# Attention with group norm on one core: every attention and q, k, v matmul in 64x64 quarters of the TensorE array

## The chip, the core and the metric

The kernel runs on one core of a Trainium2 chip. A core has TensorE (PE: matmuls, with weight loads on PEld), VectorE (DVE), ScalarE (ACT), GpSimd (POOL) and SyncE (SP, which issues most DMAs). They work side by side and wait for each other by semaphores. TensorE writes to PSUM[...]; the other data is in SBUF. The metric is the device time of the whole program in microseconds (us), lower is better; the result is the median of several runs.

## What is computed

The input x is 4 images of 512 channels and 48 x 48 = 2304 positions in float32. The reference, cut to its core:

```python
hn = _group_norm(x, gn_scale, gn_bias)            # 32 groups of 16 channels
qkv = jnp.einsum('oc,bchw->bohw', qkv_w, hn) + qkv_b[None, :, None, None]
qkv = qkv.reshape(b, 3, num_heads, d, t).astype(jnp.float16)
q, k, v = (qkv[:, 0], qkv[:, 1], qkv[:, 2])       # 8 heads, d = 64, t = 2304
scale = jnp.asarray(1.0 / math.sqrt(math.sqrt(d)), dtype=jnp.float16)
w = jnp.einsum('bhct,bhcs->bhts', q * scale, k * scale)
w = jax.nn.softmax(w, axis=-1)
a = jnp.einsum('bhts,bhcs->bhct', w, v).astype(jnp.float32)
out = jnp.einsum('oc,bchw->bohw', proj_w, a) + proj_b[None, :, None, None]
return x + out
```

## The kernel before

All of the timed work is in `fast_path`; `general_path` runs only where a flag says that a softmax sum left its safe range, and it doesn't run here. The order of the instructions is written out by hand: `tc.manual_schedule` keeps each engine's instructions in the order in which Python issues them, and pools of buffers add the waits.

**Units, blocks and pairs.** Heads go in pairs, 4 pairs for each of 4 images, so 16 pairs `g`. The queries of a pair are cut into blocks `j` of 512, 512, 512, 512 and 256 (`QBLOCKS`). A *unit* is one key tile of 128 keys for both heads against a block of 512 queries (for the block of 256, two key tiles). A unit has two parts: the scores with their exponential (`scores`, lines 920 to 940), and the product with v (`values`, 942 to 966).

- Scores (L932): the two heads lie in rows 0 to 63 and 64 to 127 of q and k, so each unit has two matmuls with 64 rows and 128 columns of the array, one for each head, into the two PSUM banks of a `ps` tile. ScalarE makes exp of the whole tile, 128 x 1024, into `p` (L939). There are three `ps` tiles (six banks).
- Product with v (L957): two matmuls with 128 rows and 64 columns, one for each head, which add up all keys of a block in one bank `av`. At the block's end DVE copies it to `avx` (L966).
- Sums of p: DVE adds the p tiles of a block (`add`, L986, L989), two matmuls with ones add the rows up (`add_up`, L1009, tile `sl`, in the bank of `av`), DVE copies it (L1025), and over DMAs, GpSimd and DVE (`check_sums`, `invert`, `spread`, `divide`) the block becomes `att`, some steps later.

**Steps.** The stream is cut into bursts of three units (`BURST`), 27 per pair, 432 in all. The main loop makes one step for each burst:

```python
scores(stream[n])
if n > 0:
    add(stream[n - 1])
if summed:
    fill(n)
if n >= BEHIND:
    values(stream[n - BEHIND])
```

So a step has three scores, then the product with v of the burst two steps back, and then (or, where a sum is due, in between) `fill(n)`, which issues work from the list `beside`: the projections of q, k and v of later pairs, the output projection of the image before, and, by `do_tasks`, statistics and normalization of the next image on DVE. `fill` spends a credit that grows with the work left over the steps left, so that each piece comes before the pair that needs it.

**Chains.** A projection is a chain of matmuls that add up the four chunks of 128 input channels in one bank, which is then evicted.

- `qk_steps` (L709): for q or k, 512 positions at a time, float32; two matmuls per chunk with 128 rows and 64 columns, into the two halves of the partitions. DVE evicts with bias and scale (L719).
- `v_chain` (L760): for v, 128 positions by 256 columns, float32, two of them to a bank; DVE adds the bias (L768).
- `proj_chain` (L837): the output projection in float32r, 128 rows and 128 columns, twice (weights split in a high and a low part); DVE adds bias and residual (L864). ScalarE casts `att` to float32r first (`att32`, L831).

In the loop these chains share one bank (`pw`), in the start they use `ps` tiles. A float32 matmul of the program is two records in the trace.

**Start and end.** The first 78 us load and normalize x of image 0 and make q, k of pair 0 and v of the first four heads, with no attention beside them. The next image's x goes into the place of the old one (`reload`), two of its blocks into spare buffers (`SPARE`). At the end the last blocks' output projections are left over.

## Time and profile before

| | |
|---|---|
| Time of the kernel, median of 3 runs | 1618.18 us (1617.79 to 1618.43) |
| The profiled execution's own time | 1618.91 us |
| Its span, first instruction to last | 1617.1 us |
| Busy PE / PEld | 1583.4 / 695.5 us |
| Busy DVE / ACT / POOL | 1136.2 / 1282.8 / 298.4 us |
| First matmul; first score | 12.8 us; 77.8 us |
| exp (L939) | 1296 times, 1231.9 us busy |
| Scores (L932) and product with v (L957) | 2880 matmuls each, 359.5 and 361.0 us busy |
| q, k (L709) and v (L760) | 2464 and 2304 records, 519.3 and 268.6 us busy |
| Output projection (L837) | 624 records in the loop, 236.6 us busy |
| DMA, mean over the span | 51 GB/s |

How to read a line of the profile: the line of the code, the engine, the operation, out<-in by the program's names, for a matmul the rows*columns of the array that it uses, the shape, and xN for N instructions. Lists of groups then give busy us and mean ns of one, and after a second bar the idle time of the engine just before them, with what ended it (<-). A timeline line begins with its start and its busy time. Matmuls are pipelined, and their ends in the trace are modelled, so that the times of neighbours overlap: the distance from one start to the next says what a matmul costs.

### The profile page before, as it was taken

How to read it: one execution, taken by the hardware profiler on the slowest of the kernel's cores; microseconds unless marked ns; L12 is line 12 of the kernel's file. 1: busy time of each engine (PE TensorE's matmuls, PEld its weight loads, DVE VectorE, ACT ScalarE, POOL GpSimd, SP SyncE). 2: the span in 40 equal slices, each digit the busy share in tenths (PEclk: the TensorE clock that was granted, in tenths of full speed). 3: DMA queues.
4: the chain of work that ended last, by engine and by line, in shares of the span. 5: the costliest groups of instructions: out<-in, count | busy, mean ns of one | idle time of the engine just before them, and what ended most of it. 6: DMA issues, size and time to landing. Idle time of an engine off the chain costs nothing.

```text
span 1617.1 us, 28315 instructions
## 1 busy us (share of the span) xinstructions
PE 1583.4 (98%) x11500; PEld 695.5 (43%) x11500; DVE 1136.2 (70%) x1302; ACT 1282.8 (79%) x1398; POOL 298.4 (18%) x419
## 2 busy tenths in 40 slices
PE   6999999999999999999999999999999999999996
PEld 2533434443333534555333353455533334434544
DVE  6267668866666678986666666898666666767775
ACT  3077777888888888888887887887888888888894
POOL 1001102211121222212111121111211131111211
PEclk9999999999999999999999999999999999999999
DMA  7002020000000023511000002352100000016424
GB/s 221 1 14 66 11 64 24 18 14 11 14 18 14 12 65 118 154 54 28 14 11 18 14 12 61 100 158 73 31 14 12 14 18 15 15 24 191 121 62 132
DMA packets 94898, 82.11 MB, mean 51 GB/s; under 512 B 50852, under 2 KB 60964, under 8 KB 94756
## 3 DMA queue, kind: packets, MB, share of 16 engines
q1 hardware_dynamic: 92724, 78.35, 17.3%
q8 instruction: 92, 1.51, 0.4%
q10 hardware_dynamic: 1904, 1.84, 0.4%
q14 instruction: 50, 0.41, 0.1%
q0 software_dynamic: 128, 0.01, 0.0%
HBM read 60.70 MB, written 19.17 MB: 49 GB/s over the span
## 4 chain that ended last, share of the span: by engine, by line
PE 91%; ACT 4%; issue 2%; DVE 1%; DMA 1%; POOL 0%; SPq 0%; ACTq 0%; DVEq 0%; POOLq 0%
PE pqk L709 29%; PE ps L932 19%; PE av L957 19%; PE pv L760 16%; PE pr L837 7%; ACT p L939 3%; PE ps L709 1%; PE sl L1009 1%; ACT a L831 1%; DMA x<-x_dram 1%; DVE acc L986 0%; DMA sums<-slx 0%; DVE r L860 0%; DMA row<-inv 0%; DMA ib<-row 0%
## 5 line engine op out<-in xcount | busy, mean ns | idle before, releaser
L939 ACT ACTIVATE p<-ps 128x1024 f16<-128x1024 f32 x1296 | 1231.9, 1027 | 299.9 <-PE ps L932 299.3
L986 DVE TENSOR_TENSOR acc<-acc,p 128x3072 f16<-128x3072 f16 x270 | 485.3, 1798 | 75.5 <-ACT p L939 74.7
L709 PE MATMUL pqk<-x,wqkv 128*64 128x512 f32 (+1 forms) x2464 | 519.3, 551 | 0.0
L932 PE MATMUL ps<-q,k 64*128 64x512 f16 (+1 forms) x2880 | 359.5, 358 | 6.2 <-ACT p L939 5.3
L957 PE MATMUL av<-p,v 128*64 128x512 f16 (+1 forms) x2880 | 361.0, 364 | 0.4 <-DVE slx L1025 0.3
L760 PE MATMUL pv<-wqkv,x 128*64 128x256 f32 x2304 | 268.6, 380 | 0.0
L709 PEld LDWEIGHTS pqk<-x,wqkv 128*64 128x64 f32 x2464 | 168.9, 137 | 224.2 <-issue 166.8
L1047 POOL TENSOR_SCALAR in<-sums 128x8 f32<-128x8 f32 (+1 forms) x158 | 116.6, 738 | 795.0 <-DMA sums<-slx 788.7
L932 PEld LDWEIGHTS <-k 64*128 64x128 f16 x2880 | 107.3, 94 | 286.1 <-issue 238.1
L957 PEld LDWEIGHTS <-v 128*64 128x64 f16 x2880 | 131.9, 109 | 210.8 <-issue 166.6
L1073 POOL TENSOR_TENSOR att<-avx,ib 128x512 f16<-128x512 f32 (+1 forms) x78 | 120.0, 1539 | 450.4 <-DMA ib<-row 406.3
L760 PEld LDWEIGHTS pv<-wqkv,x 128*64 128x64 f32 x2304 | 160.1, 137 | 92.8 <-issue 4.5
L986 DVE TENSOR_TENSOR acc<-p,p 128x3072 f16<-128x3072 f16 x79 | 138.2, 1749 | 0.0
L837 PE MATMUL pr<-a,whi 128*128 128x512 f32 (+1 forms) x312 | 122.2, 399 | 4.6 <-DVE r L860 3.2
L837 PE MATMUL pr<-a,wlo 128*128 128x512 f32 (+1 forms) x312 | 114.4, 373 | 0.0
L989 DVE TENSOR_TENSOR acc<-acc 128x1024 f16<-128x1024 f16 x156 | 108.4, 695 | 5.4
L719 DVE TENSOR_SCALAR q<-pqk,bqkv 128x512 f16<-128x512 f32 (+1 forms) x79 | 55.0, 696 | 80.4 <-PE pqk L709 79.8
L719 DVE TENSOR_SCALAR k<-pqk,bqkv 128x512 f16<-128x512 f32 (+1 forms) x75 | 52.2, 696 | 78.1 <-PE pqk L709 78.0
L768 DVE TENSOR_TENSOR v<-pv,bv 128x512 f16<-128x512 f32 x72 | 49.7, 691 | 81.1 <-PE pv L760 80.9
L966 DVE COPY avx<-av 128x512 f32<-128x512 f32 (+1 forms) x79 | 50.6, 641 | 66.4 <-PE av L957 66.4
L864 DVE SCALAR_TENSOR_TENSOR r<-pr,bproj,r 128x512 f32<-128x512 f32 (+1 forms) x80 | 54.9, 694 | 43.6 <-PE pr L837 43.0
L837 PEld LDWEIGHTS pr<-a,whi 128*128 128x128 f32 x312 | 58.5, 187 | 41.9 <-issue 18.7
(62 smaller groups left out, 448.8 us busy)
## 6 DMA issues: line engine op xcount, KB each, us to landing
r<-x_dram SPq DMA_DIRECT2D x72, 256.0 KB, 3.0
out_dram<-r SPq DMA_DIRECT2D x69, 256.0 KB, 2.1
ib<-row SPq DMA_DIRECT2D x126, 128.0 KB, 3.0
x<-x_dram SPq DMA_DIRECT2D x62, 256.0 KB, 4.3
x<-x_dram SPq DMA_DIRECT2D x16, 128.0 KB, 4.8
sums<-slx SPq DMA_DIRECT2D x128, 2.0 KB, 2.1
ib<-row SPq DMA_DIRECT2D x30, 64.0 KB, 3.0
wqkv<-qkv_wT_dram SPq DMA_DIRECT2D x2, 768.0 KB, 6.9
```

Source lines behind the costliest of these rows:

```text
L709: nc.tensor.matmul(pw[0][lo : lo + D, :n], wqkv[:, c, w0 + lo : w0 + lo + D], hn[b, c, j], start=(c == 0), stop=(c == NC - 1),)
L719: nc.vector.tensor_scalar(qk[g][part][:, o : o + n], pw[0][:, :n], bqkv[:, col : col + 1], SCALE, ALU.add, ALU.mult,)
L760: nc.tensor.matmul(pw[0][lo : lo + D, a, :], hn[b, c, i * P // QB][:, at + lo : at + lo + D], wqkv[:, c, 2 * C + half * C // 2 :][:, : C / ...
L837: nc.tensor.matmul(ps[:, :n], w[:, c, bass.ts(m, P)], at32[b, j, c], start=(i == 0), stop=(i == len(steps) - 1),)
L864: nc.vector.scalar_tensor_tensor(xt[:, i], places[i], bias, xt[:, i], ALU.add, ALU.add)
L932: nc.tensor.matmul(ps[:, h, a * n : (a + 1) * n], kt[rows, bass.ts(i, P)], qt[rows, o : o + n], start=True, stop=True,)
L939: nc.scalar.activation(pt[:, r], ps, AF.Exp)
L957: nc.tensor.matmul(av[0][lo : lo + D, :n], vv[b, pr // 2][:, i, pr % 2 * P + lo : pr % 2 * P + lo + D], pt[:, r, h, a * n : (a + 1) * n], ...
L986: nc.vector.tensor_tensor(t, before, pt, ALU.add)
L989: nc.vector.tensor_tensor(t[:, 0], t[:, 0], t[:, r], ALU.add)
L1047: nc.gpsimd.tensor_scalar(t, sm, limit, None, op)
L1073: nc.gpsimd.tensor_tensor(atts[g][:, o : o + n], avx.pop((g, j))[:, :n], ibs.pop((g, j))[:, :n], ALU.mult,)
```

## The change

The scores, the product with v and the projections of q, k and v all use the array in quarters of 64 rows and 64 columns. Of the two uses with more rows, the sums (`add_up`, 128 rows, 64 columns) and the output projection (128 x 128) stay as they were.

- **Scores**: four matmuls for a unit, each head's 128 keys in two halves of 64 (`score`). The `ps` tiles go from three to two.
- **Product with v**: four matmuls for a unit; the keys of a tile are cut into two halves, and each half of the rows adds up in its own bank, so `av` takes two banks. At the end of a block `join` copies one bank to `avx` on ScalarE and adds the other on DVE.
- **Chains of q, k and v** are 256 columns wide (`CW`), and each is cut in two by rows: in one *slot* it is run with rows 0 to 63 for all four chunks, in the next slot with rows 64 to 127, beside the first half of the next chain (`merged`, `slot`). Two banks, `pw0` and `pw1`, take turns. A chain without a partner is run alone; `settle` puts a small matmul and a DVE copy ahead of that.
- **Steps**: a step has at most one slot, cut in halves, and scores and products alternate unit by unit: score, product, score, product, half of the slot, score, product, rest of the slot. Where a sum is due it comes first, then two scores, half of the slot, the products. A burst has two or three units (`BURSTS`): 3, 3, 2, 3, 2, 3, 2 for a block of 512 queries, 2, 2, 2, 3 for one of 256; 511 steps in all. A whole output chain may take a slot.
- **Around it**: the sum, check, spread and divide of a block are due 3, 5, 7 and 9 steps after its last burst (`lag`). The next image's statistics are made from temporary loads (`stats_ahead`, in the buffers of `att32`), so its x is loaded twice and no spare buffers are needed. Casts are queued one by one (`do_cast`).

The diff, cut to what the text speaks of:

```diff
+BURSTS = {QB: (3, 3, 2, 3, 2, 3, 2), T % QB: (2, 2, 2, 3)}
+LAST_BURSTS = (3, 3, 3)
+CW = QB // 2
...
-    ps_s = ctx.enter_context(tc.tile_pool(name="ps_s", bufs=3, space=PSUM))
+    ps_s = ctx.enter_context(tc.tile_pool(name="ps_s", bufs=2, space=PSUM))
...
+    def chain_bank(name):
+        at = 1 - (last_bank[0] if held[0] is None else held[0])
+        last_bank[0] = at
+        return ps_w.tile([P, QB], F32, tag=f"pw{at}", name=name)
...
+        def step(c, row):
+            rows = rows_of_array(row)
             for lo in (0, D):
                 nc.tensor.matmul(
                     pw[0][lo : lo + D, :n],
-                    wqkv[:, c, w0 + lo : w0 + lo + D],
-                    hn[b, c, j],
-                    start=(c == 0),
-                    stop=(c == NC - 1),
+                    wqkv[rows, c, w0 + lo : w0 + lo + D],
+                    hn[b, c, j][rows, off : off + n],
+                    start=(c == 0 and not row),
+                    stop=(c == NC - 1 and row != 0),
                 )
...
+        ps = ps_s.tile([P, 2, QB], F32, tag="ps", name=f"ps_{g}_{j}_{k}_{r}")
+        for a in range(per):
+            i = (at + r) * per + a
+            for lo in (0, D):
+                for h in range(2):
+                    rows = slice(h * D, (h + 1) * D)
+                    nc.tensor.matmul(
+                        ps[lo : lo + D, h, a * n : (a + 1) * n],
+                        kt[rows, i * P + lo : i * P + lo + D],
+                        qt[rows, o : o + n],
...
+            for half in range(2):
+                keys = slice(half * D, (half + 1) * D)
+                for h in range(2):
+                    lo = h * D
+                    at_v = pr % 2 * P + lo
+                    nc.tensor.matmul(
+                        av[0][lo : lo + D, half, :n],
+                        vv[b, pr // 2][keys, i, at_v : at_v + D],
+                        pt[keys, r, h, a * n : (a + 1) * n],
...
+    def join(to, banks, n):
+        nc.scalar.copy(to, banks[:, 0, :n])
+        nc.vector.tensor_tensor(to, banks[:, 1, :n], to, ALU.add)
...
+        if before and not (chain and before.followed):
+            settle()
+            if not chain:
+                settle()
+        if chain:
+            chain.open()
...
+        steps = merged(chain, before)
+        yield from in_halves(steps, max(at + us for at, _, us, _ in steps) / 2)
+        pending[0] = chain
+        if before:
+            closed(before)
...
+        return ((3, 5, 7, 9) if stream[n][0] < NG - 2 else (3, 4, 5, 6))[step]
...
+        summed = list(blocks(n, 0))
+        for found in summed:
+            rows(*found, add_up(*found))
...
+        part = begin_slot(n)
         if summed:
-            rows(*summed, add_up(*summed))
...
+            issue([ss], 2)
+            if n > 0:
+                add(stream[n - 1])
+            if part:
+                next(part)
+            issue([vs], 2)
+            issue([ss, vs], 1)
+        else:
+            issue([ss, vs], 2)
+            if n > 0:
+                add(stream[n - 1])
+            if part:
+                next(part)
+            issue([ss, vs], 1)
+        in_order()
...
+        finish(part)
```

## The prediction

> **What bounds the kernel now.** I read the page first: the busy times, then the chain that ended last.

> ```profile
> PE 1583.4 (98%) x11500; PEld 695.5 (43%) x11500; DVE 1136.2 (70%) x1302; ACT 1282.8 (79%) x1398; POOL 298.4 (18%) x419
> ...
> PE 91%; ACT 4%; issue 2%; DVE 1%; DMA 1%; POOL 0%; SPq 0%; ACTq 0%; DVEq 0%; POOLq 0%
> ```

> TensorE is on 91% of the chain, so only its time counts: what its matmuls take and what lies between them. The timeline of PE over one step, with a block's sum (sl) in it, shows both (start, busy us):

> ```profile
> 601.74 0.82 PE L932 MATMUL ps<-q,k 64*128 64x512 f16 x6
> 602.49 0.84 PE L957 MATMUL av<-p,v 128*64 128x512 f16 x6
> 603.16 1.88 PE L709 MATMUL pqk<-x,wqkv 128*64 128x512 f32 x8
> 604.88 0.38 PE L1009 MATMUL sl<-acc,ones 128*64 128x512 f16 x2
> 605.20 0.82 PE L932 MATMUL ps<-q,k 64*128 64x512 f16 x6
> ```

> Busy times overlap, so I take differences of starts. At 2.4 columns per ns six score matmuls, two side by side, need 3 x 0.213 = 0.64 us, but the next run starts 0.75 later: 0.11 over. av to pqk: 0.67, 0.03 over. pqk (2 x 0.853 = 1.71) to sl: 1.72, nothing over. sl (0.21) to ps: 0.32, 0.11 over. So the array runs at full rate except where the number of rows changes, between 64*128 and 128*64; there it loses 0.11 us. f16 to f32 in one shape is nearly free. Such a pair of matmuls starts every 0.216 us.

> ScalarE over the same time, then PE and ScalarE where a step had no projection in it:

> ```profile
> 602.17 2.86 ACT L939 ACTIVATE p<-ps 128x1024 f16<-128x1024 f32 x3 [0.38 <-PE ps L932]
> ...
> 629.12 0.82 PE L957 MATMUL av<-p,v 128*64 128x512 f16 x6
> 629.87 0.89 PE L932 MATMUL ps<-q,k 64*128 64x512 f16 x4
> 631.28 0.39 PE L932 MATMUL ps<-q,k 64*128 64x512 f16 x2 [0.52 <-ACT p L939]
> 631.61 0.84 PE L957 MATMUL av<-p,v 128*64 128x512 f16 x6
> ```

> The first exp starts 0.43 after its score (602.17 - 601.74). Three take 2.86, the last alone 1.03, so one follows another by 0.915. A step of three without a projection is 1.3 us of PE against 2.75 of exps: PE waits for ScalarE (the 0.52), today seldom (12 waits, 5.3 us). Normally the projection's 1.7 us cover the exps, and three score buffers let PE run ahead.

> For the prices, DVE at a block's end and three rows of the groups by shape:

> ```profile
> 603.44 0.69 DVE L966 COPY avx<-av 128x512 f32<-128x512 f32 x1 [0.78 <-PE av L957]
> ...
> 605.30 0.69 DVE L1025 COPY slx<-sl 128x512 f32<-128x512 f32 x1
> ...
> L719 DVE TENSOR_SCALAR q<-pqk,bqkv 128x512 f16<-128x512 f32 x63 | 47.3, 750 | 71.6 <-PE pqk L709 71.1
> ...
> L831 ACT CAST a<-att 128x512 fp32r<-128x512 f16 x64 | 35.2, 639 | 2.7 <-POOL att L1036 2.3 <-PE pr L837 0.5
> ...
> L719 DVE TENSOR_SCALAR q<-pqk,bqkv 128x256 f16<-128x256 f32 x16 | 7.7, 480 | 8.8 <-PE pqk L709 8.7
> ```

> av is copied out by DVE alone, right after its last matmul and beside the next projection; the sum comes 1.4 us later and finds the bank free.

> [...]

> **Part by part.** The sum is made against the profiled run's 1618.9 us (span 1617.1, 1.8 around it), 0.7 above the median of 1618.2. Counts of the changed kernel come from the order in which it issues.

> 1. Shape changes of the array: 955 before, 400 after (what stays: whole projections of the output in 128*128, and the sums in 128*64). 555 x 0.115 = **-64**.

> 2. Matmul work. Scores and av become 11,520 quarter matmuls, four per unit instead of two per unit; 12,672 f32 records of 64x256, eight per chunk of two chains. If four quarters run at once, a score or av unit is 0.216 and a chain's slot 8 x 0.216 = 1.73, the same array time as now. Bounds: 0 if they overlap; 396 slots x 1.73 = +683 if the f32 row halves don't. I take 0: two tiles overlap fully now, in rows (ps) and in columns (av). Blocks of 256 queries have loads twice as dense as any seen: 0 to +61 (2304 x 0.107 / 4); I take 0. 128 of the f32 records run with the other half empty (a chain that has no partner): 128 x 0.213 / 4 = **+7**.

> 3. The end of a block. The step in which av's last matmul falls is now: score, av, score, av, half slot, score, half slot: 5 x 0.216 + 1.73 = 2.80 us. ScalarE has in its queue exp, exp, then the copy, then the third exp. Exp 1 starts at 0.43, exp 2 at 1.35, ending at 2.37; the copy (0.6, by the 0.639 of the cast) ends at 2.9, the DVE add (0.69) at 3.6 with handoffs. PE's next instruction is the sum, which takes av's banks, and nothing passes it: all later scores wait. It comes at 2.80 and waits 0.85. Before or after the short block (step of 2.59, or the copy behind three exps) it is 1.1: mean 0.95. It hits 79 blocks. Nine of these steps have no slot to cover any of it, 1.7 more each: 79 x 0.95 - 5 (slots of the output projection, longer) + 9 x 1.2 (a part is in point 4's kind of wait) = **+81**. Bounds: 0, if the copy gets ahead of exp 2, to +110.

> 4. Steps without a slot. 511 steps (17 of three units and 15 of two per head pair) hold about 396 slots of q, k, v and 71 steps with an output projection; 49 are empty, nine counted above. Score buffers fall from three to two. An empty step of three: 2.75 + 0.15 handoffs - 1.29 = 1.6; of two: 1.83 + 0.1 - 0.86 = 1.1. 28 x 1.6 + 12 x 1.1 = **+58**. The step before cannot lend time, as two buffers let ScalarE be at most two exps behind.

> 5. Banks of the chains. Two banks alternate; a chain's eviction (0.48 for 256 columns) must end before the slot after the next opens, 0.86 us into a step. On DVE it stands behind an add of up to 1.75 us, started only when the last exp of the step before is done, and a 0.63 task. 3.0 us of step usually hold 0.4 + 1.75 + 0.48, not with two tasks. Bounds 0 to +70 (0.7 in 100 steps); I take **+30**.

> 6. Engines that stay off the path: ScalarE +79 x 0.6 = +47 (1283 to 1330); DVE +56 (twice as many evictions at 0.48 instead of 0.75: 22 for q and k, 15 for v; 79 more adds: 19), to about 1190; 60 more loads of x on SP, hidden, since DMA is 17% busy. Waits of PE for exps that the kernel before has go: **-5**.

> Sum: 1618.9 - 64 + 7 + 81 + 58 + 30 - 5 = 1726; less 0.7, **1725**.

> **Rivals.**
> A, the forecast: PE saves 64 on shape changes and gives over twice that back in new waits; about 1725, by the bounds of 3 and 5 from 1650 to 1800.
> B, faster: the join and the exps don't hold PE. If the copy were done by 2.2 us into the step, point 3 is gone; if steps without a slot fall where ScalarE is idle anyway, most of 4. Then 1618.9 - 64 + 7 + 20 = 1582. The page speaks for it in that ScalarE is idle 299.9 us before exps today; against it, this idle time lies at the start of each step and the copy stands behind exps of the same step. It decides from waits below 57 us in all; I count 169.
> C: the f32 row halves run one after the other: 1725 + 683, less some 90 of waits that the longer slots cover: about 2320. For it: no trace shows four quarters. Against: both kinds of two-way tiling are at full rate.
> D: the quarters overlap but 256-column blocks are limited by loads, or halves start skewed: 1725 + 61 = 1786.
> E: gains and waits cancel, 1615 to 1621.

> **Numbers.** A 0.67, B 0.17, C 0.08, D 0.05, E 0.03. Faster by over 0.2% (what a measurement can tell here) 0.17, within 0.03, slower 0.80. A alone: 1650 to 1800. To leave out no more than 2 in 10, C and most of B, the range goes from 1600 to 1810.

> **What would show it.** In the changed trace: ps to av without the 0.11 (right for 1); a chain's slot of 1.73 in two halves of 0.86 (wrong at 3.4: C); PE idle before sl of 0.7 to 1.1, put down to DVE avx, some 75 us in all (3); PE idle before ps put down to ACT, 60 to 80 us (4); PE idle before pqk and pv put down to DVE (5). PE's share of the chain falls below 90%, and ACT and DVE rise. If sl starts within 0.2 us of the step's last matmul, point 3 is wrong, and the kernel is faster if 4 shrinks too.

## The result and the profile after

The changed kernel takes 1738.86 us (median of 4 runs, 1738.57 to 1743.03) against 1618.15 us, a ratio of 1.0752 with a 95% interval of 1.0733 to 1.0771: slower by 121 us. The profiled execution is the slowest of the four, 1743.03 us with a span of 1741.3.

The page of the changed kernel, busy times and the chain that ended last:

```profile
PE 1591.8 (91%) x25526; PEld 964.4 (55%) x25526; DVE 1185.0 (68%) x1586; ACT 1329.2 (76%) x1478; POOL 244.6 (14%) x419
...
PE 66%; DVE 13%; ACT 12%; issue 5%; DMA 2%; POOL 1%; SPq 0%; ACTq 0%; DVEq 0%; POOLq 0%
```

PE is busy for almost the same time as before (1583.4), but holds only two thirds of the chain; DVE and ACT have come onto it with 25%. So PE's work hasn't grown, it is waited for. Its timeline, from one full step to the next (start, busy us):

```profile
700.87 0.39 PE L943 MATMUL ps<-q,k 64*64 64x512 f16 x4
701.08 0.39 PE L970 MATMUL av<-p,v 64*64 64x512 f16 x4
...
701.51 0.39 PE L970 MATMUL av<-p,v 64*64 64x512 f16 x4
701.73 1.90 PE L710 MATMUL pqk<-x,wqkv 64*64 64x256 f32 x32
703.46 0.39 PE L943 MATMUL ps<-q,k 64*64 64x512 f16 x4
```

Four quarters run at full rate: a score and a product each take 0.21 from start to start, 32 float32 records 1.73. Nothing is lost between ps, av and pqk. What is lost stands in the list of PE's waits (us, times, longest):

```profile
PE ps L943 <- ACT p L950: 49.8, 111, 5.4
PE sl L1033 <- DVE avx L985: 41.3, 52, 2.6
...
PE pqk L710 <- DVE q L720: 8.4, 12, 2.4
PE pv L754 <- DVE v L763: 7.0, 14, 0.8
PE pr L852 <- DVE r L868: 5.4, 8, 1.3
```

These leave out part of each wait, since the ends of matmuls are modelled. I therefore measure *in starts*: the distance from one start to the next, less what the matmuls need at the rate of the traces (512 columns in 0.216 us, 2.4 per ns) and the 0.11 that a change of shape took in the trace before; what is over 0.2 us counts as a wait of the later matmul. "Chains" are pqk, pv, pr and settle together.

| waits of PE after 78 us, in starts | for exps (ps) | sl | chains | time, us |
|---|---|---|---|---|
| before | 8 | 0 | 6 | 1618 |
| changed | 80 | 47 | 51 | 1739 |
| 1 join on DVE | 79 | 14 | 48 | 1704 |
| 2 464 steps | 22 | 65 | 65 | 1717 |
| 3 add last | 228 | 92 | 32 | 1923 |
| 4 the three together | 162 | 150 | 40 | 1930 |
| 5 add last, some | 85 | 93 | 32 | 1765 |
| 6 products first | 89 | 8 | 50 | 1706 |
| 7 products first, 464 steps, add last | 24 | 100 | 31 | 1720 |
| 8 before with two score buffers | 473 | 0 | 3 | 2081 |
| 9 as 6, short adds last | 93 | 14 | 28 | 1692 |
| 10 as 9, 464 steps | 34 | 6 | 34 | 1634 |
| 11 as 10, projections later | 30 | 6 | 29 | 1626 |
| 12 as 11, last two pairs | 25 | 7 | 30 | 1624 |

A step without a slot, then a block's end, on PE, ScalarE and DVE of the changed kernel:

```profile
710.58 0.41 PE L943 MATMUL ps<-q,k 64*64 64x512 f16 x4 [0.48 <-ACT p L950]
...
715.45 0.41 PE L1033 MATMUL sl<-acc,ones 128*64 128x512 f16 x2 [0.47 <-DVE avx L985]
```

```profile
709.50 4.69 ACT L950 ACTIVATE p<-ps 128x1024 f16<-128x1024 f32 x5 [0.65 <-PE ps L943]
714.04 0.63 ACT L984 COPY avx<-av 128x512 f32<-128x512 f32 x1
```

```profile
714.70 0.69 DVE L985 TENSOR_TENSOR avx<-av,avx 128x512 f32<-128x512 f32 x1 [2.32 <-ACT avx L984]
```

ScalarE makes five exps without a pause while PE waits for buffers, and only then the copy; DVE has been idle for 2.32 us, adds for 0.69, and the sum starts. Through the whole run DVE waits 158.5 us in that place (79 times): nobody works there while the copy stands in ScalarE's queue.

### The profile page after: what moved, and what is told of

Its sections match the earlier page's. It is cut to its first block, busy times and chain, and to the rows that moved or that the text cites. A ratio compares the mean times of both kernels' runs of the same rounds, so it can differ in the third digit from the quotient of the medians.

```text
span 1741.3 us, 57021 instructions
## 1 busy us (share of the span) xinstructions
PE 1591.8 (91%) x25526; PEld 964.4 (55%) x25526; DVE 1185.0 (68%) x1586; ACT 1329.2 (76%) x1478; POOL 244.6 (14%) x419
## 4 chain that ended last, share of the span: by engine, by line
PE 66%; DVE 13%; ACT 12%; issue 5%; DMA 2%; POOL 1%; SPq 0%; ACTq 0%; DVEq 0%; POOLq 0%
PE pqk L710 22%; PE ps L943 12%; PE pv L754 12%; PE av L970 10%; ACT p L950 10%; PE pr L852 7%; DVE acc L1006 5%; DVE acc L1013 3%; DVE avx L985 2%; PE sl L1033 2%; ACT avx L984 1%; PE ps L710 1%; DMA ib<-row 1%; DMA r<-x_dram 1%; DVE r L868 1%
## 5 line engine op out<-in xcount | busy, mean ns | idle before, releaser
L710 PE MATMUL pqk<-x,wqkv 64*64 64x256 f32 (+1 forms) x8704 | 584.6, 381 | 14.5 <-DVE q L720 8.4
L943 PE MATMUL ps<-q,k 64*64 64x512 f16 (+1 forms) x5760 | 509.3, 362 | 50.4 <-ACT p L950 49.8
L1006 DVE TENSOR_TENSOR acc<-acc,p 128x2048 f16<-128x2048 f16 (+1 forms) x349 | 504.4, 1445 | 27.1 <-ACT p L950 26.8
L970 PE MATMUL av<-p,v 64*64 64x512 f16 (+1 forms) x5760 | 495.0, 359 | 1.2 <-DVE slx L1046 1.2
L710 PEld LDWEIGHTS pqk<-x,wqkv 64*64 64x64 f32 (+1 forms) x8704 | 325.1, 134 | 188.8 <-DVE q L720 33.1
L943 PEld LDWEIGHTS <-k 64*64 64x64 f16 x5760 | 193.5, 106 | 219.3 <-issue 136.3
L754 PE MATMUL pv<-wqkv,x 64*64 64x256 f32 (+1 forms) x4320 | 302.0, 379 | 10.7 <-DVE v L763 7.0
L754 PEld LDWEIGHTS pv<-wqkv,x 64*64 64x64 f32 (+1 forms) x4320 | 174.6, 133 | 101.4 <-DVE v L763 25.5
L970 PEld LDWEIGHTS <-v 64*64 64x64 f16 x5760 | 179.1, 108 | 92.6 <-issue 11.0
L985 DVE TENSOR_TENSOR avx<-av,avx 128x512 f32<-128x512 f32 (+1 forms) x80 | 51.1, 638 | 158.6 <-ACT avx L984 158.5
L1006 DVE TENSOR_TENSOR acc<-p,p 128x3072 f16<-128x3072 f16 (+1 forms) x79 | 130.1, 1647 | 0.0
```

Of the source, the lines that this page charges most:

```text
L710: nc.tensor.matmul(pw[0][lo : lo + D, :n], wqkv[rows, c, w0 + lo : w0 + lo + D], hn[b, c, j][rows, off : off + n], start=(c == 0 and not row),
L754: nc.tensor.matmul(pw[0][lo : lo + D, : C // 2], hn[b, c, j][rows, at + lo : at + lo + D], wqkv[rows, c, 2 * C + half * C // 2 :][:, : C / ...
L943: nc.tensor.matmul(ps[lo : lo + D, h, a * n : (a + 1) * n], kt[rows, i * P + lo : i * P + lo + D], qt[rows, o : o + n], start=True, stop=True,
L970: nc.tensor.matmul(av[0][lo : lo + D, half, :n], vv[b, pr // 2][keys, i, at_v : at_v + D], pt[keys, r, h, a * n : (a + 1) * n], start=(i = ...
L985: nc.vector.tensor_tensor(to, banks[:, 1, :n], to, ALU.add)
L1006: nc.vector.tensor_tensor(t[:, :m], before[:, :m], pt[:, :m], ALU.add)
```

## The experiments

My theory: three new waits, of the sum, of the score buffers and of the chains' banks, eat what the shape changes save. Rivals: DVE's or ScalarE's load; quarters that are slow in themselves; waits that only change places.

**1. The join's copy on DVE.**

```diff
-        nc.scalar.copy(to, banks[:, 0, :n])
+        nc.vector.tensor_copy(to, banks[:, 0, :n])
```

> The changed kernel with one word altered: the first half of join is copied on DVE instead of ScalarE, so that it doesn't stand behind an exp. Against the changed kernel's 1739 us. Theory (new waits at the block's end): PE's waits ahead of sl for DVE avx, about 47 us in starts over the block ends, go to under 10; DVE's 80 copies of 0.69 fall into its own idle time of 2 us there, so 1690 to 1705. Rival 1 (DVE is the engine that holds the kernel back): 55 us more on DVE, so 1745 or more. Rival 2 (waits only move: the exps of the same step are late instead): the waits for exps grow by what the sums lose, 1730 to 1740.

1704.21 us, ratio to the kernel before 1.0534 (1.0517 to 1.0552). sl's waits fall from 47 to 14, a little less than expected, and the others stay. With 47 us more on DVE (1185.0 to 1232.1) the kernel is 35 us faster, so rival 1 falls, and rival 2 for this wait.

**2. Fewer steps.**

```diff
-BURSTS = {QB: (3, 3, 2, 3, 2, 3, 2), T % QB: (2, 2, 2, 3)}
+SEVEN = (3, 3, 2, 3, 2, 3, 2)
+BURSTS = {j: SEVEN if j in (1, 3) else (3,) * 6 for j in range(4)}
+BURSTS[4] = (3, 3, 3)
```

> The changed kernel cut into 464 steps instead of 511: blocks 0, 2 and 4 of a pair in bursts of three units only. Steps without a slot of a chain fall from 49 to 13 (12 of three units), all in the last two pairs. Theory (a step without a slot leaves ScalarE behind, and two score buffers let PE get only two exps ahead): PE's waits for exps fall from 80 us in starts to some 25 to 35; 1739 - 50 = about 1690. A rival: the waits come from the two score buffers in every step, with or without a slot; then they stay at 80 or grow, since more of the steps have three units, 1735 to 1760. If the time is lost because the quarters themselves are slow, nothing changes either.

1716.60 us, 1.0609 (1.0591 to 1.0627). The waits for exps fall from 80 to 22 as expected, so they do come from steps without a slot. But 32 of the 58 us come back, in sl and in the chains:

```profile
PE sl L1035 <- DVE avx L987: 59.6, 56, 2.5
...
PE ps L945 <- ACT p L952: 12.0, 27, 1.3
```

A block that ends in a burst of three has its last product one half slot later in the step, and the copy behind it. The trace shows it by blocks: the sums of blocks 0 and 2, which now end so, wait 1.32 and 1.37 on average instead of 0.57 and 0.34, those of blocks 1 and 3, left as they were, 0.24 and 0.15 instead of 0.25 and 0.71. The rival is wrong, but what neither side expected is seen: a wait that goes uncovers another.

**3. The add behind the eviction.**

```diff
-            if n > 0:
+            if n > 0 and ended(n - BEHIND):
                 add(stream[n - 1])
...
         finish(part)
+        if n > 0 and not ended(n - BEHIND):
+            add(stream[n - 1])
```

> The changed kernel with DVE's add of the p tiles issued at the end of the step, behind the eviction of the chain that ends there, and not before it (in the step of a block's last product the order stays). Theory (chain banks wait for evictions that stand behind an add): PE's waits ahead of pqk, pv and pr, about 50 us in starts, fall to under 20; 1739 - 35 = about 1704. Rival: the evictions are late because DVE has too much to do or because the bank turns round too fast by itself; then 1735 to 1745, and the waits are still put down to q, k and v on DVE.

1922.95 us, 1.1886 (1.1867 to 1.1906): a miss of 220 us. The chains' waits fall from 51 to 32, but ScalarE has a wait that it didn't have (its list of waits):

```profile
ACT p L950 <- DVE acc L1006: 229.3, 79, 5.7
```

The first add of a block reads the p tiles of its first two bursts. Moved to the end of its step, it holds the first one so long that the fourth burst, which needs this buffer (there are three), waits 2.9 us, once in each block. My edit, not the theory, was at fault; I hadn't counted what the add frees.

**4. The three edits together.**

> All three edits in one kernel: join on DVE, 464 steps, add behind the eviction. Theory (three separate waits that add up): 1739 - 40 - 50 - 35 = about 1615, at or a little below the kernel before; a bit less if, as before, an overlap of the waits makes the sum smaller: 1600 to 1640. Rival (quarters are slower in themselves, or the waits feed on each other): above 1680.

1929.52 us, 1.1931 (1.1886 to 1.1977). It contains the edit of experiment 3 and shows no more than that; inconclusive on the sum of the three.

**5. The same, without the add that holds p.**

```diff
+    def soon_read(n):
+        return ended(n - BEHIND) or stream[n - 1][2] == 1
...
-            if n > 0:
+            if n > 0 and soon_read(n):
                 add(stream[n - 1])
...
         finish(part)
+        if n > 0 and not soon_read(n):
+            add(stream[n - 1])
```

> As the third experiment (DVE's add behind the eviction), but the add that reads the first two p tiles of a block stays where it was, as does the one in the step of a block's last product. In the third experiment ScalarE waited 229 us for DVE acc at 79 places, once for each block, because that add holds the first p tile and there are three. Theory: with that gone, what is left is the effect that was sought; PE's waits ahead of pqk and pv fall from 38 us in starts to 15, in 5 of 7 steps; 1739 - 20 = about 1719. Rival (p buffers are short also behind the other adds): ScalarE's waits for DVE acc stay above 30 us, 1740 to 1780.

1765.13 us, 1.0905 (1.0887 to 1.0923): again slower than the changed kernel, though ScalarE's wait for DVE is gone and the chains' waits are at 32. Now sl waits 93, at 78 of 79 places. Experiment 7 has the same edit and shows the cause best.

**6. The products first.** The copy stays on ScalarE, one place further ahead.

```diff
-            issue([ss, vs], 2)
+            if v and v[3]:
+                issue([ss], 1)
+                issue([vs], v[5])
+                issue([ss], 1)
+            else:
+                issue([ss, vs], 2)
```

> The changed kernel with one order altered: in the step of a block's last product, all products are issued after the first score, so that ScalarE has the copy of join behind one exp and not behind two. No work is added or moved to another engine. Theory (the copy's place in ScalarE's queue is what sl waits for): sl's waits, 47 us in starts, go to under 10, as with the copy on DVE; 1739 - 40 = about 1700. Rival (it is ScalarE's load: its exps are late in these steps, so the copy is late anywhere, or the exps behind it become late by 0.6 us): 1725 to 1740, with the waits for exps up by 20 to 40 us.

1706.21 us, 1.0542 (1.0524 to 1.0559), sl's waits at 8, exps' at 89. No work was taken from ScalarE, so it was the place in its queue; the rival's extra wait for exps is 9 us, not 20 to 40.

**7. Products first, 464 steps and the edit of 5.**

> The changed kernel with 464 steps, the products first in a block's last step, and the add behind the eviction where it holds no p tile. Theory: the three waits are separate once the join no longer depends on the burst's length; PE's waits for exps 22 us as in the second experiment, ahead of sl under 10, of the chains about 30: 1739 - 58 - 37 - 16 = about 1628, range 1605 to 1650; at or a little above the kernel before. Rival (each wait that goes lets another take its place): 1670 or more.

1720.50 us, 1.0634 (1.0616 to 1.0652), a miss. Waits for exps and chains came as expected (24 and 31), sl's are 100. DVE at the end of a block:

```profile
714.71 0.48 DVE L722 TENSOR_SCALAR q<-pqk,bqkv 128x256 f16<-128x256 f32 x1 [0.87 <-PE pqk L712]
715.11 1.98 DVE L1008 TENSOR_TENSOR acc<-acc,p 128x2048 f16<-128x2048 f16 x1
717.12 1.42 DVE L1015 TENSOR_TENSOR acc<-acc 128x1024 f16<-128x1024 f16 x2
718.46 0.68 DVE L987 TENSOR_TENSOR avx<-av,avx 128x512 f32<-128x512 f32 x1
```

Behind the eviction (714.71) now come 3.4 us of adds, and right after them, without a gap, the join's add. Moved out of the evictions' way, the adds stand in the join's way: in 74 of 76 waits of sl, such an L1015 stands directly ahead of the join. In the sixth kernel, where the adds stand in the old place, 33 waits of chains (21 us) have the same two short adds directly ahead of the eviction.

**8. The kernel before with two score buffers.**

```diff
-    ps_s = ctx.enter_context(tc.tile_pool(name="ps_s", bufs=3, space=PSUM))
+    ps_s = ctx.enter_context(tc.tile_pool(name="ps_s", bufs=1, space=PSUM))
...
-            ps = ps_s.tile([P, 2, QB], F32, tag="ps", name=f"ps_{g}_{j}_{k}_{r}")
+            ps = ps_s.tile([P, 2, QB], F32, tag=f"ps{turn()}", name=f"ps_{g}_{j}_{k}_{r}")
```

> The kernel before, whole, with scores in two ps tiles instead of three (the third tile is used at the start and the end alone). No quarters, no join, no new chains: the price of the third score buffer alone, in the order of three scores, then three products. The third score of a step then waits until the first exp of the step is done, about 0.43 + 1.03 us into it, 1.0 us later than before: with 432 steps up to 430 us, less where the exps of the step before ran late anyway. Theory (the number of score buffers sets how far PE may go ahead, and the changed kernel's alternation of score and product is what keeps its loss at 80): 1850 to 2050. Rival (two buffers are enough and the changed kernel's waits for exps come from its steps alone): below 1660.

2080.62 us, 1.2855 (1.283 to 1.2881), 30 us beyond the range. PE in one step:

```profile
802.49 0.61 PE L936 MATMUL ps<-q,k 64*128 64x512 f16 x4
804.05 0.39 PE L936 MATMUL ps<-q,k 64*128 64x512 f16 x2 [0.96 <-ACT p L943]
```

The third score starts 1.56 us after the first instead of 0.43: 1.1 us in each of 432 steps, 473 in all. The third buffer is worth 462 us in the old order. The changed kernel, whose second av bank and second chain bank take its place in PSUM, waits only 72 us more for exps than the kernel before. That this is because it alternates score, product and half slots fits these numbers, but no run changes the alternation alone.

**9. Only the short adds behind the eviction**, with the products first.

```diff
+            tails.append((t, parts))
+            acc[g, j] = [t[:, :1]]
...
+    def add_tails():
+        while tails:
+            t, parts = tails.pop()
             for part in parts:
                 nc.vector.tensor_tensor(t[:, 0], t[:, 0], part, ALU.add)
-            acc[g, j] = [t[:, :1]]
...
         finish(part)
+        add_tails()
```

> The sixth experiment (products first in a block's last step, copy on ScalarE) and one more order: the two or three short adds at the end of a block (128x1024, 0.71 us each) are issued at the end of their step, behind the eviction of the chain; the large adds stay where they were. In the sixth experiment 33 of the waits for a chain's bank, 21 us in starts, had just such an add right ahead of the eviction on DVE, and in the fifth and seventh it stood ahead of the join's add. Theory (the place of that one add in DVE's queue decides): the waits for banks fall by some 20 us and sl's stay under 12, as the join's add comes only at 2.1 us of the next step; 1706 - 18 = about 1688. Rival (any add that is moved delays the join): sl's waits above 40 us, 1710 or more.

1692.46 us, 1.0462 (1.0445 to 1.0480). The chains' waits fall from 50 to 28, sl's rise from 8 to 14: the place of that one pair of adds is what decided.

**10. All three orders.** Experiment 9 with the steps of experiment 2.

> The three orders together: 464 steps, products first in a block's last step, short adds behind the eviction. Theory: waits for exps 22 us in starts, for sl under 12, for banks about 25; 1739 - 58 - 36 - 22 = about 1623, range 1605 to 1645: all that the changed kernel lost in waits beyond what the kernel before had, less some 60, is then given back, and it stands within a per cent of the kernel before. Rival (a wait that goes makes room for another): above 1660.

1633.82 us, 1.0097 (1.0080 to 1.0114). The waits for exps, sl and chains add to 74 instead of 178. Its chain that ended last, and its waits:

```profile
PE 79%; ACT 9%; DVE 5%; issue 4%; DMA 1%; POOL 0%; SPq 0%; DVEq 0%; ACTq 0%; POOLq 0%
```

```profile
PE ps L945 <- ACT p L952: 18.4, 55, 1.3
...
PE sl L1042 <- DVE avx L987: 4.4, 9, 0.9
```

The 464 steps bring 59 us here (1692 to 1634) and brought 22 alone: there sl's waits rose from 47 to 65 and the chains' from 51 to 65, here they go from 14 to 6 and from 28 to 34, as the join no longer depends on the burst's length.

**11. The third image's output projections later.**

```diff
-        places = (2, 12, 22, 32, 42) if b < B - 1 else (8, 20, 32, 44, 54)
+        places = (2, 12, 22, 32, 42) if b < B - 1 else (24, 34, 44, 50, 54)
```

> As the tenth, and the output projections of the third image come later in the list, so that more work is left for the last two pairs: 10 steps without a slot instead of 13, those of three units. Theory: 3 steps fewer at 1.5 us: 4 to 6 us less than the tenth, 1618. If the end is bound by something else (the last exps, the DMA of the residuals), no change.

1625.89 us, 1.0050 (1.0033 to 1.0066). Waits for exps 34 to 30, chains 34 to 29.

**12. The last two pairs.** There all bursts have three units, and DVE copies the join's first half.

```diff
+SEVENS = {14: (), 15: ()}
...
+        copy = nc.scalar.copy if g < NG - 2 else nc.vector.tensor_copy
+        copy(to, banks[:, 0, :n])
```

> As the eleventh, and for the last two pairs alone: all bursts of three units (7 steps without a slot instead of 10, 460 steps in all), and the first half of join copied on DVE. In the eleventh, PE still waits 19 us in starts for exps there, of 30 in all; the rest of its waits is some 40 us spread over the run. Theory: 3 steps at 1.5 us and 9 copies of 0.6 us that ScalarE no longer makes where it is the bound: 1626 - 8 = about 1618, level with the kernel before; within 0.3% of it in either direction. Rival (the end is bound by the length of the exps alone): no change, 1624 to 1628.

1623.69 us (1621.45 to 1626.38), 1.0036 (1.0023 to 1.0050). Against the eleventh this is 2 us less, with times that overlap (1624.57 to 1627.53 there), so the rival, no change, isn't excluded. It is the lowest time of the quarters here, and still 5 us behind the kernel before. By the table it has 62 us of waits where the kernel before has 14, and 410 shape changes instead of 954: 48 us more against 60 us less. Two smaller things keep it from being faster. From the first score on, the columns of all its matmuls take 7 us more (1378.3 us against 1371.5, those side by side counted once), since some chains run alone in half of the array. And gaps of under 0.2 us each are some 15 us more in all, 6 of them ahead of scores and 6 ahead of the output projections; why they are there was not found out.

## Why the prediction held, point by point

The forecast was 1725 and slower; the time is 1739. Spans compared, 1741.3 - 1617.1 = 124 us were added, where the sum had 107. The kinds of waits came as forecast, their sizes did not: point 3 was 34 us too high, points 4 and 5 together 34 us too low. That these errors cancel is luck.

| point | forecast | measured |
|---|---|---|
| 1 shape changes | -64 | 954 to 399, by 0.11: -61 |
| 2 quarters, halves alone | 0 and +7 | full rate; columns of all matmuls from the first score on, 1371.5 to 1377.1: +6 |
| 3 block end | +81 | 47 - 0 = +47 |
| 4 steps without a slot, with -5 for the old waits for exps | +53 | 80 - 8 = +72 |
| 5 chains' banks | +30 | 51 - 6 = +45 |
| not in the sum: half clock | none | up to +16, part of it inside the rows above |
| not in the sum: gaps under 0.2 us | none | +15 |

Counted from the starts of all matmuls with nothing in two rows, the 124 us are about 152 of waits, 15 of half clock, 15 of small gaps and 6 of columns, less 61 of shape changes and 2 at the start and the end.

Point 1 and the full rate of point 2, for which before had no line to read, came as taken. Rivals C and D fall with them.

Point 3 was right in its mechanism. The copy starts 1.61 us after the last product (median), which is the forecast's 1.65 (2.30 into the step less 0.65), and experiments 1 and 6 remove the wait in two ways. Its size was too large: the forecast gave 0.95 to each end with a slot, and the trace has 0.45 on average for 56 ends with a slot of q, k or v, and 0.18 for 14 with an output projection; only the 9 without a slot, as many as forecast, are at 1.98, near the forecast's 0.95 + 1.2. The term that was sized wrongly is that points 3 and 5 were added as if they fell in different steps. Of the 56 ends, 25 have no wait for a chain's bank in their step, and there the sum waits 0.77; in the other 31 the chains wait 0.62 and the sum only 0.18. PE at an end without a wait:

```profile
100.98 0.41 PE L970 MATMUL av<-p,v 64*64 64x512 f16 x4
102.16 1.09 PE L710 MATMUL pqk<-x,wqkv 64*64 64x256 f32 x16 [0.76 <-DVE k L720]
...
104.27 0.41 PE L1033 MATMUL sl<-acc,ones 128*64 128x512 f16 x2
```

The half slot waits 0.76 for its bank, and under this wait copy and add end in time. Both waits lie in the same step, since the short adds of a block come just before; so the forecast's 81 + 30 = 111 is 92 in the trace, and in experiment 5 the chains' waits fall by 19 while sl's rise by 46.

Point 4 is confirmed by experiment 2, at 72 instead of 53. Point 5 named the wrong add for the largest part: not the add of up to 1.75 us in every step, but the two short ones behind the last add of a block. In the trace 35 waits for a chain's bank, 21 of the 51 us, have such a short add directly ahead of the eviction, and experiment 9, which moves only these, takes 22 us off the chains' waits of experiment 6. Point 6 held: ScalarE 1329.2 of the forecast 1330, DVE 1185.0 of about 1190, and 47 us more on DVE cost nothing in experiment 1.

Rival B was to win with new waits below 57 us. Experiment 10 comes near and 11 and 12 get there (60, 51 and 48 more than the kernel before, by the table), and the time comes to within 1.0, 0.5 and 0.4% of the kernel before, not below it: the mark of 57 left out the small gaps. So the gain on shape changes is real, and two thirds of the new waits were a matter of order and of the cut into steps, not of quarters. Whether the rest can be removed stays open.

## What to carry to other kernels

Price a layout by the banks that it takes: here a saving of 61 us on shape changes took the two banks of the third score buffer and a join of two banks, and the waits that came with both and with the new order cost more. Where an instruction joins an engine's queue (the copy above started at 714.04, behind five exps), write down what stands ahead of it and what waits behind it in that same step, and what each moved instruction frees; moving adds on DVE gave anything from a loss of 184 us to a gain of 14. Don't add waits of one step: the first that comes can cover much of the next, 0.77 to 0.18 us here.

## What the runs showed of the hardware

```profile
1619.57 0.64 PE L1033 MATMUL sl<-acc,ones 128*64 128x256 f16 x4 [1.92 <-DVE avx L985]
...
1622.28 0.64 PE L943 MATMUL ps<-q,k 64*64 64x512 f16 x4
1622.70 0.64 PE L970 MATMUL av<-p,v 64*64 64x512 f16 x4
```

```profile
180.00:182.00 2.00, 1.49 (x24) 0.93 (x27) 1.97 (x5) 0.69 (x2) 0.00 (x0) 0.94 0.05 8
182.00:184.00 2.00, 2.00 (x24) 0.98 (x20) 2.00 (x2) 1.25 (x2) 0.00 (x0) 0.50 0.27 65
184.00:186.00 2.00, 2.00 (x32) 1.09 (x28) 0.63 (x2) 0.14 (x1) 0.39 (x2) 0.71 0.21 52
186.00:188.00 2.00, 2.00 (x44) 1.25 (x40) 1.84 (x3) 2.00 (x3) 1.46 (x3) 1.00 0.83 210
```

At 1622.28 a score takes 0.42 from start to start, not 0.21; the stretch from 182 follows a sum that waited 1.93. Shares of 0.94, 0.50 and 0.71 in three stretches of 2 us are 3.4 us at half clock ((0.06 + 0.50 + 0.29) x 2 / 0.5). PE's busy time in such stretches, times the missing share of the clock, is 16 us between 80 us and the end in the changed kernel, 32 in experiment 3, and 0 in the kernel before and in experiment 11; the 432 waits of 1.1 us in experiment 8 left the clock at 0.998. The forecast had priced waits at their length alone.

The length of one wait doesn't decide. Six of the nine falls in the changed kernel follow a sum that waited 1.7 to 2.6 us at a block's end without a slot; the other three lie in the last 60 us. Three more sums that waited 1.7 or 1.8 (at 203, 225 and 1720 us) and a chain that waited 2.4 (at 439) were followed by no fall. What tells them apart in this trace is where they lie. In its record of the granted clock all nine falls lie a whole number of 3.413 us apart (the second is 19 steps after the first at 181.76, the third 83), and the clock stays at 0.50 for 3.413 us after five of them, for 6.827 after three, and to the end after the last. In the step of 3.413 us just ahead of each fall matmuls took 0.23 to 0.34 of the time, by their starts and columns; of all such steps at full clock between 80 us and the last matmul, counted from the first fall, the emptiest without a fall has 0.37. So in this trace one and the same wait cost or not with what else filled its step; why the clock falls was not shown.
